# Cross-attention and FFN on one core: stacked 128-row score products, halves staged ahead, FFN by weight column groups

## The chip, the cores and the metric

One core of a Trainium2 chip runs the whole program. The metric is the device time of one launch in microseconds, and less is better. TensorE (PE) does matrix products into PSUM, VectorE (DVE), ScalarE (ACT) and GpSimd (POOL) do elementwise work, and SyncE (SP) issues nearly all transfers (DMA). Each engine takes its instructions in order and waits on semaphores.

## The reference

```
x = x + xattn(layernorm(x), ctx, mask, mask, Wq, bq, Wk, bk, Wv, bv)     # x: (16, 256, 512)
x = x + ffn(layernorm(x), lut, gate_idx, up_idx, down_idx)

xattn: 16 heads of 16 rows; q = Wq t + bq, k = Wk s + bk, v = Wv s + bv, each (16, 256, 512)
       dot = q.T k / 4 per head (512 x 512);  m = mask_t * mask_s
       amap = softmax(m * dot - (1 - m) * 1e6) * m;  out = amap v
ffn:   w = lut[idx] for gate, up (1376 x 512) and down (512 x 1376), lut of 16 entries
       out = (silu(x gate.T) * (x up.T)) down.T
```
All arrays are float32. The layer norm runs over the 512 columns. Rows of the FFN are the 16 x 256 rows of x.

## The kernel before

**Units and steps.** A group k (0 to 31) is half the heads of one batch: 8 heads of 16 rows. It has two units u = 2k + e, each with 4 heads (even or odd ones). A unit has 4 column chunks c of 128; a step is one chunk and two heads, so a unit is 8 steps and there are 512. At step s, `quad(a, p)` (L403 to L436) makes two score blocks of 128 x 1024: pa for a unit 12 steps ahead (AHEAD = 12), of which DVE takes the row maximum (L434), and pb, the transposed block of the unit at hand, of which ACT takes the exponential (L436). The three buffers of `ps_sc` are shared by pa and pb.

**A score block is three products.** TensorE's fast float32r form keeps fewer bits than float32, so q and k are cut into halves (high bits, rest). Each head has 32 rows: `qs`, `ks` hold (high, rest), `qx`, `kx` the swapped order. A block adds ks x qs, kx x qs and a product of mask rows (`ka`, `qa`), and for pb the rows `qm` with the maximum. Each product is 32 rows tall; two heads of pa and two of pb sit in four different row groups, and the order written out is n (product), jj (head), pa then pb.

**Staging.** `project` (L332 to L356) makes q or k of a group in float32, POOL multiplies the mask, `halve` (L250) cuts, and three transfers (L355) write the halves to a DRAM tile of 8 heads x 48 rows. `spread` (L358 to L370) reads them back: per unit four copies of 256 KB into 128 rows (L363, L364) and two of mask rows (L368). `turn_max` (L438 to L449) turns the maxima on TensorE and sends them to `qm` in four transfers (L448). `apply_v` (L452) multiplies by v in float32, 4 heads in 4 column groups, once every second step; of the 32 columns of a head 16 are ones and give the softmax sums.

**Rows.** `take_sums` (L478), `merge` (L484), `invert` (L488), `send_sums` (L493), `spread_sums` (L498, L504) and `finish_rows` (L510 to L512) bring the sums of a group together, divide, add x and write x2 to DRAM. All of these transfers, the staging, the loads of the next batch (`load_b`), of rows for the statistics of layer norm (`load_xs`, L233) and of the index tables (L559) are issued on SP's one queue, in the order of the step table (`after`, `lumps`, from L515).

**Order.** `manual_schedule` keeps the order as written. The table fixes at which step each piece stands; `fill_step` gives DVE a credit of 0.39 us of table look-ups per step, which turn the indices into the gate and up weights (`wg`, `wu`, kept in SBUF).

**FFN.** 8 blocks of 512 rows. `gate_up(n)` runs over 11 column groups o of the weights, 8 products of 128 x 128 x 512 in float32 each (two matmul records per product), Silu on ACT, a product on DVE; `down(n)` runs 4 x 11 products and adds x2. The rows of block n + 1 are normed and turned inside `gate_up(n)`. The down weights are looked up during the first two blocks. Block 0 starts beside the last attention steps.

Of the kernel before, what the change touches and what calls it, by code (L numbers as in the profile page):

```python
# [9 lines left out]
F32 = mybir.dt.float32  # L10
I32 = mybir.dt.int32
F32R = mybir.dt.float32r
HALF = -4096
# [8 lines left out]
def kernel(  # L22
# [17 lines left out]

# [15 lines left out]
    AHEAD = 12  # L70
    NSTEP = 8 * NU
    PIECE = INTER // 4
# [4 lines left out]
    wpool = ctx.enter_context(tc.tile_pool(name="ffnw", bufs=1))  # L77
    rpool = ctx.enter_context(tc.tile_pool(name="res", bufs=2))
    xpool = ctx.enter_context(tc.tile_pool(name="xT", bufs=1))
    dpool = ctx.enter_context(tc.tile_pool(name="dram", bufs=1, space=DRAM))  # L80
    ps_m = ctx.enter_context(tc.tile_pool(name="ps_m", bufs=1, space=PSUM))
# [3 lines left out]
    eps = cpool.tile([P, 1], F32, tag="eps", name="eps")  # L85
    nc.vector.memset(eps, EPS)
    lut_b = cpool.tile([P, LUT], F32, tag="lut", name="lut_b")
    lut_x = cpool.tile([P, LUT // 2], I32, tag="lutx", name="lut_x")
    wg = wpool.tile([P, NH, INTER], F32, tag="wg", name="wg")
    wu = wpool.tile([P, NH, INTER], F32, tag="wu", name="wu")  # L90
    x2_d = [dpool.tile([P, T], F32, tag=f"x2_{k}", name=f"x2_{k}") for k in range(NK)]

# [5 lines left out]
    def row_rstd(mv, rstd, nmr):  # L98

        nc.scalar.activation(rstd, mv[:, :, 1], AF.Sqrt, bias=eps)  # L100
        nc.vector.reciprocal(rstd, rstd)
        nc.vector.scalar_tensor_tensor(nmr, mv[:, :, 0], -1.0, rstd, ALU.mult, ALU.mult)

    lut_i = lut_b.bitcast(I32)

    def look_up(pool, dst, it, name):

# [7 lines left out]
        m, ops = [], []  # L115

        def low():
            m.append(new("b0"))
            v.tensor_scalar(m[0], it, 31, 31, ALU.logical_shift_left, ALU.arith_shift_right)

        def bit(i):
            m.append(new(f"b{i}"))
            v.tensor_scalar(m[i], it, 1 << i, None, ALU.bitwise_and)

        ops.append(low)
        for i in range(1, 4):
            ops.append(lambda i=i: bit(i))
# [10 lines left out]

        ops.append(lambda: leaf(0, d))
# [12 lines left out]
        ops.append(lambda: join(2, 4, 6))  # L152
        ops.append(lambda: join(3, 0, 4))
        return ops

    xTs, odd = {}, []

    def load_x2(pool, n, t):
        xt = pool.tile([P, T], F32, tag="x2", name=f"x2_{n}_{t}", bufs=4)
        nc.sync.dma_start(xt, x2_d[4 * n + t])  # L160
        return xt

    def prep_stats(pool, n):

        mv = pool.tile([P, 4, 2], F32, tag="mv", name=f"mv_{n}")
        rstd = pool.tile([P, 4], F32, tag="rs", name=f"rs_{n}")
        nmr = pool.tile([P, 4], F32, tag="nr", name=f"nr_{n}")
        xts = [load_x2(pool, n, t) for t in range(4)]
        for t in range(4):
            row_stats(pool, mv[:, t, :], xts[t], f"f{n}_{t}")  # L170
        row_rstd(mv, rstd, nmr)
        xTs[n] = (odd[0] if n % 2 else xpool).tile([P, NH, 4 * P], F32, tag="xT", name=f"xT_{n}")
        xns = {}

        def norm(t):
            xns[t] = pool.tile([P, T], F32, tag="xn2", name=f"xn2_{n}_{t}", bufs=2)
            nc.vector.tensor_scalar(
                xns[t], xts[t], rstd[:, t : t + 1], nmr[:, t : t + 1], ALU.mult, ALU.add
            )

        def turn(t):
            pt = ps_m.tile([P, 512], F32, tag="m", name=f"pt_{n}_{t}")
            xn = xns.pop(t)
            for h in range(NH):
                nc.tensor.transpose(
                    pt[:, h * P : (h + 1) * P], xn[:, h * P : (h + 1) * P], ident
                )
            nc.scalar.copy(
                xTs[n][:, :, t * P : (t + 1) * P], pt.rearrange("p (h r) -> p h r", r=P)
            )  # L190

        return norm, turn


    with ExitStack() as att:
        ac = att.enter_context(tc.tile_pool(name="att_const", bufs=1))
        p1 = att.enter_context(tc.tile_pool(name="att1", bufs=1))
        p2 = att.enter_context(tc.tile_pool(name="att2", bufs=2))
        pp = att.enter_context(tc.tile_pool(name="att_p", bufs=2))
        lp = att.enter_context(tc.tile_pool(name="lookup", bufs=1))  # L200
        ps_sc = att.enter_context(tc.tile_pool(name="ps_sc", bufs=3, space=PSUM))
        ps_pv = att.enter_context(tc.tile_pool(name="ps_pv", bufs=1, space=PSUM))

# [8 lines left out]
        m_d = dpool.tile([B, 4, T], F32, tag="m_d", name="m_d")  # L212
        mcomp = ac.tile([P, B, 32], F32, tag="mcomp", name="mcomp")
        mv1 = ac.tile([P, NK, 2], F32, tag="mv1", name="mv1")
        rstd1 = ac.tile([P, NK], F32, tag="rstd1", name="rstd1")
        nmr1 = ac.tile([P, NK], F32, tag="nmr1", name="nmr1")
        qss, qxs, kss, kxs = [
            [ac.tile([P, T], F32R, tag=f"{w}{i}", name=f"{w}{i}") for i in range(3)]
            for w in ("qs", "qx", "ks", "kx")
        ]  # L220
        qms = [ac.tile([P, T], F32R, tag=f"qm{i}", name=f"qm{i}") for i in range(3)]
        qas = [ac.tile([P, T], F32R, tag=f"qa{i}", name=f"qa{i}") for i in range(2)]
        kas = [ac.tile([P, T], F32R, tag=f"ka{i}", name=f"ka{i}") for i in range(2)]
        vas = [ac.tile([P, NCH, HEADS, 32], F32, tag=f"va{i}", name=f"va{i}") for i in range(2)]

        def x_of(b):
            return x[b].rearrange("(o p) t -> p o t", p=P)

        def load_xs(b):
            xs = []  # L230
            for o in range(NCC):
                t = p2.tile([P, T], F32, tag="xs", name=f"xs_{b}_{o}", bufs=1)
                nc.sync.dma_start(t, x_of(b)[:, o, :])  # L233
                xs.append(t)
            return xs

        def words(t):
            return t.bitcast(F32)

        def spread_mask(b):  # L240

            ka, qa = words(kas[b % 2]), words(qas[b % 2])
            for n in range(2):
                nc.sync.dma_start(ka[1 + n : P : 16, :], m_d[b, n].partition_broadcast(8))
                for h in range(2):
                    nc.sync.dma_start(
                        qa[1 + n + 16 * h : P : 32, :], m_d[b, 2 + h].partition_broadcast(4)
                    )

        def halve(hi, lo, t, eng):  # L250
            nc.vector.tensor_scalar(
                hi.bitcast(I32), t.bitcast(I32), HALF, None, ALU.bitwise_and
            )
            eng.tensor_tensor(lo, t, hi, ALU.subtract)

        def stats1(b, xs):
            for o in range(NCC):
                row_stats(p2, mv1[:, b * NCC + o, :], xs[o], f"a{b}_{o}")

        def rstd1_of(lo, hi):  # L260
            at = slice(lo * NCC, hi * NCC)
            row_rstd(mv1[:, at, :], rstd1[:, at], nmr1[:, at])
# [3 lines left out]
        def load_b(b):  # L266
            cx = p2.tile([P, NCC, T], F32, tag="ctx", name=f"ctx_{b}")
            nc.sync.dma_start(cx, src[b].rearrange("(o p) t -> p o t", p=P))
            xn = p2.tile([P, NCC, T], F32, tag="xn", name=f"xn_{b}")
            nc.sync.dma_start(xn, x_of(b))  # L270
            mb = p2.tile([P, T], F32, tag="mb", name=f"mb_{b}")
            nc.sync.dma_start(mb, mask[b, 0].partition_broadcast(P))
            inp[b] = (cx, xn, mb)

        def norm1(b, eng):
            xn = inp[b][1]
            for o in range(NCC):
                i = b * NCC + o
                eng.tensor_scalar(
                    xn[:, o, :], xn[:, o, :], rstd1[:, i : i + 1], nmr1[:, i : i + 1],  # L280
# [8 lines left out]
        nc.scalar.dma_start(bkc, bk.rearrange("(o p) -> p o", p=P))  # L289
        nc.scalar.dma_start(mrow, mask.rearrange("b o (c p) -> (b o c) p", p=P))  # L290
# [7 lines left out]
        for t in qms + qas:  # L298
            nc.gpsimd.memset(t.bitcast(F32), 0.0)
        for t in kas:  # L300
            nc.vector.memset(t.bitcast(F32), 0.0)
        ones = wg[:8, 3, :T]
        nc.vector.memset(ones, 1.0)
        for t in kas:
            nc.sync.dma_start(words(t)[0:P:16, :], ones)
        for t in vas:
            nc.gpsimd.memset(t, 1.0)
        stats1(0, [inp[0][1][:, o, :] for o in range(NCC)])
        rstd1_of(0, 1)
        norm1(0, nc.vector)  # L310
        nc.vector.tensor_scalar(bqc, bqc, QK, None, ALU.mult)
        mm = wg[:B, 0, :T]
        nc.scalar.dma_start(mm, mask[:, 0, :])
        for n, (by, op) in enumerate(((-1.0, ALU.add), (NEG, ALU.mult))):
            m, hi = wg[:B, 1 + n, :T], wg[:B, 1 + n, T : 2 * T]
            nc.vector.tensor_scalar(m, mm, by, None, op)
            halve(hi, m, m, nc.vector)
            nc.sync.dma_start(m_d[:, 2 * n, :], hi)
            nc.sync.dma_start(m_d[:, 2 * n + 1, :], m)
        spread_mask(0)  # L320
# [9 lines left out]
        nat, mbank = {}, {}  # L330

        def project(k, which, o):  # L332
            b, oc = divmod(k, NCC)
            cx, xn, mb = inp[b]
            w, src_t = (wk, cx) if which == "k" else (wq, xn)
            if o == 0:
                mbank[0] = ps_m.tile([P, 512], F32, tag="m", name=f"p{which}_{k}")
            nc.tensor.matmul(
                mbank[0], w[:, o, oc * P : (oc + 1) * P], src_t[:, o, :],
# [437 lines left out]
```

## Time and profile before

| what | us |
|---|---|
| median of 2 runs (2801.1 to 2802.07) | 2801.59 |
| the profiled execution | 2809.51 |
| its span, first to last instruction | 2807.7 |
| PE busy | 2148.9 |
| DVE busy | 1195.1 |
| ACT busy | 740.4 |
| POOL busy | 414.1 |

A page of the profile has the busy time of each engine, the same in 40 slices of 70 us (digits are tenths; PEclk is the clock granted to TensorE, DMA the busy share of the 16 DMA engines), the chain of waits that ended last, the costliest groups of instructions by line (count, then busy us and mean ns of one, then idle time ahead of them and what ended it), and the transfers. Groups name tiles: `pa<-ks,qs` writes pa from ks and qs. Float32 products of 128 rows pass at 8 records in 3.43 us when TensorE is full. The reduce of L434 takes 1222 ns each (512 of them), the exponential of L436 1023 ns (512).

### The profile page before, as it was taken

To read this page: it belongs to the slowest core of one execution; us is meant where nothing else is said; L and a number is where in the kernel's file an instruction comes from. 1 tells how busy PE (TensorE), PEld (TensorE's weight loads), DVE (VectorE), ACT (ScalarE), POOL (GpSimd) and SP (SyncE) were. 2 spreads that over 40 slices of the span, in tenths; PEclk is the share of its full clock that TensorE was granted. 3 is DMA by queue.
4 is the path that set the end of the run, shared out by engine and by line. 5 is a ranking of instruction groups with operands and counts; after the bars stand their busy time and mean duration, and the time that the engine had idled before them with its cause. 6 is when DMAs were issued, how large, how long until landed. Compare 5 with 4: busy or idle time off the path is not lost.

```text
span 2807.7 us, 28960 instructions
## 1 busy us (share of the span) xinstructions
PE 2148.9 (77%) x11009; PEld 926.4 (33%) x11009; DVE 1195.1 (43%) x1903; ACT 740.4 (26%) x892; POOL 414.1 (15%) x435
## 2 busy tenths in 40 slices
PE   1666655577677676767767667679999999999999
PEld 0322222233232232223223223233444444444444
DVE  2545455455455555555555555548811111111100
ACT  0233333243343333333333333341101011010100
POOL 2221111122122222212212222100000000000000
PEclk6677777788787877878878878899999999999999
DMA  3232333333333333333333332311011101011000
GB/s 118 84 107 91 121 105 92 107 93 110 115 91 114 109 91 107 106 97 111 104 103 107 93 114 91 97 59 34 26 38 38 45 0 45 12 34 45 4 26 15
DMA packets 135162, 217.83 MB, mean 78 GB/s; under 512 B 26736, under 2 KB 33840, under 8 KB 135024
## 3 DMA queue, kind: packets, MB, share of 16 engines
q1 hardware_dynamic: 133008, 214.73, 23.8%
q8 instruction: 87, 1.43, 0.2%
q10 hardware_dynamic: 1760, 0.99, 0.2%
q14 instruction: 51, 0.42, 0.0%
q0 software_dynamic: 256, 0.26, 0.0%
HBM read 140.26 MB, written 67.76 MB: 74 GB/s over the span
## 4 chain that ended last, share of the span: by engine, by line
PE 52%; DMA 31%; SPq 7%; DVE 4%; ACT 2%; issue 2%; POOL 2%; ACTq 0%; POOLq 0%; DVEq 0%
DMA qs<-dq 15%; PE po L697 11%; PE pg L679 10%; PE pu L679 10%; DMA dq<-natq 8%; PE pa L429 8%; PE pv L460 5%; DMA qx<-dq 4%; PE pb L429 3%; SPq L448 2%; PE pv L380 2%; SPq L355 1%; DMA xs<-in_x_dram 1%; ACT pt L436 1%; DVE nm L434 1%
## 5 line engine op out<-in xcount | busy, mean ns | idle before, releaser
L434 DVE TENSOR_REDUCE nm<-pa 128x2 f32<-128x1024 f32 x512 | 625.5, 1222 | 682.1 <-PE pb L429 526.3
L436 ACT ACTIVATE pt<-pb 128x1024 f32<-128x1024 f32 x512 | 523.6, 1023 | 1030.7 <-PE pb L429 866.9
L429 PE MATMUL pa<-ks,qs 32*128 32x512 f32 x1024 | 376.3, 575 | 509.4 <-DMA qs<-dq 435.7
L429 PEld LDWEIGHTS pa<-ks,qs 32*128 32x128 f32 x1024 | 168.1, 212 | 848.0 <-issue 641.9
L460 PE MATMUL pv<-pt,va 128*32 128x512 f32 x2048 | 350.1, 763 | 3.8 <-ACT pt L436 3.8
L679 PE MATMUL pg<-xT,wg 128*128 128x512 f32 (+1 forms) x704 | 320.8, 599 | 0.0
L679 PE MATMUL pu<-xT,wu 128*128 128x512 f32 (+1 forms) x704 | 316.5, 592 | 0.0
L429 PE MATMUL pb<-qs,ks 32*128 32x512 f32 x1024 | 297.0, 575 | 25.2 <-ACT pt L436 15.8
L429 PE MATMUL pa<-kx,qs 32*128 32x512 f32 x1024 | 313.9, 468 | 0.0
L429 PE MATMUL pa<-ka,qa 32*128 32x512 f32 x1024 | 307.0, 456 | 0.0
L697 PE MATMUL po<-wd,ht 128*128 128x512 f32 (+1 forms) x704 | 303.4, 592 | 0.0
L429 PE MATMUL pb<-qm,ka 32*128 32x512 f32 x1024 | 237.9, 457 | 54.3 <-DMA qm<-mx 54.3
L686 DVE TENSOR_TENSOR ht<-sg,pu 128x512 f32<-128x512 f32 (+1 forms) x88 | 60.4, 686 | 413.4 <-PE pu L679 410.3
L429 PE MATMUL pb<-qx,ks 32*128 32x512 f32 x1024 | 234.8, 452 | 0.0
L684 ACT ACTIVATE sg<-pg 128x512 f32<-128x512 f32 (+1 forms) x88 | 52.3, 596 | 650.0 <-PE pg L679 649.9
L697 PEld LDWEIGHTS po<-wd,ht 128*128 128x128 f32 (+1 forms) x704 | 133.7, 190 | 168.8 <-issue 168.8
L679 PEld LDWEIGHTS pu<-xT,wu 128*128 128x128 f32 (+1 forms) x704 | 132.1, 188 | 170.1 <-issue 169.6
L679 PEld LDWEIGHTS pg<-xT,wg 128*128 128x128 f32 (+1 forms) x704 | 131.6, 190 | 159.4 <-issue 158.2
L429 PEld LDWEIGHTS pa<-ka,qa 32*128 32x128 f32 x1024 | 176.4, 225 | 11.8
L389 POOL TENSOR_TENSOR vt<-vt,bvb 128x256 f32<-128x256 f32 x64 | 45.8, 739 | 906.4 <-ACT vt L386 906.4
L429 PEld LDWEIGHTS pa<-kx,qs 32*128 32x128 f32 x1024 | 152.0, 225 | 0.0
L702 DVE TENSOR_TENSOR ob<-po,x 128x512 f32<-128x512 f32 x32 | 22.1, 691 | 279.7 <-PE po L697 279.7
(96 smaller groups left out, 1883.1 us busy)
## 6 DMA issues: line engine op xcount, KB each, us to landing
dk<-hik SPq DMA_DIRECT2D x64, 256.0 KB
dq<-hiq SPq DMA_DIRECT2D x64, 256.0 KB
ks<-dk SPq DMA_DIRECT2D x64, 256.0 KB
kx<-dk SPq DMA_DIRECT2D x64, 256.0 KB
qs<-dq SPq DMA_DIRECT2D x64, 256.0 KB
qx<-dq SPq DMA_DIRECT2D x64, 256.0 KB
x<-x SPq DMA_DIRECT2D x64, 256.0 KB
ctx<-in_ctx_dram SPq DMA_DIRECT2D x16, 512.0 KB
```

Source lines behind the costliest of these rows:

```text
L355: nc.sync.dma_start(d[:, r : r + 16, :], f)
L380: nc.tensor.matmul(ps[:, i * C : (i + 1) * C], cx[:, o, c * P : (c + 1) * P], wv[:, o, :], start=(o == 0), stop=(o == NCC - 1),)
L389: nc.gpsimd.tensor_tensor(vt[:, cc], vt[:, cc], bvb, ALU.add)
L429: nc.tensor.matmul(ps[:, jj, :], w[at, cc * P : (cc + 1) * P], m[at, :], start=(n == 0), stop=(n == 2),)
L434: nc.vector.tensor_reduce(nms[u][:, c, h : h + 2], pa, AX.X, ALU.max, negate=True)
L436: nc.scalar.activation(pts[u2, c2][:, h2 : h2 + 2, :], pb, AF.Exp)
L448: nc.sync.dma_start(words(qms[u % 3])[0:P:16, c * P : (c + 1) * P], mx[8 * c : 8 * c + 8, :])
L460: nc.tensor.matmul(accs[u][32 * j : 32 * j + 32, :], va[:, c, 8 * oc + 2 * j + e, :], pt[:, j, :], start=(c == 0), stop=(c == NCH - 1),)
L679: nc.tensor.matmul(ps[:rows], w[:, h, at], xT[:, h, :], start=(h == 0), stop=(h == NH - 1),)
L684: nc.scalar.activation(sg[:rows], pg[:rows], AF.Silu)
L686: nc.vector.tensor_tensor(ht[:rows], sg[:rows], pu[:rows], ALU.mult)
L697: nc.tensor.matmul(po, ht[:rows, t * P : (t + 1) * P], wd[:rows, o, :], start=(o == 0), stop=(o == NO - 1),)
```

## The change

**Scores.** A head's rows are stacked to 128: rows 0 to 31 and 32 to 63 hold the halves, 64 to 67 the mask rows, 126 and 127 the two halves of the maximum; the rest is zero in Q and one in K. A block is then one product per head of 126 (pa) or 128 (pb) rows, 4 matmuls a step where there were 12. Q and K are four tiles each, of 128 x 4 x 512. pa and pb no longer alternate: pa's two, then pb's two. AHEAD is 14. `apply_v` runs two chunks every fourth step, with three `pt` buffers.

**Staging.** The high half is made by an ACT copy to float32r, the rest on POOL. `stage` writes a half in two transfers per group and side; `fetch_unit` reads a unit 8 steps before its first pa. `turn_max` sends two transfers, `take_sums` one, `send_sums` two.

**Layer norm.** Its root is a power on POOL, not Sqrt on ACT; statistics are taken from `load_b`'s own tile. Each group's rows are normed and turned inside the attention loop (`stats2`, `norm2`, `turn_rows`) and written to DRAM as `xT_d`.

**FFN.** Looked-up gate and up weights go to DRAM (`w_d`), half of the columns during attention (0.26 us of credit a step), the rest and the down weights during gate/up (3.8 us of credit per group and block). Gate/up runs over column groups o outside and row blocks n inside, with all 8 xT blocks in SBUF; each h piece is written to DRAM (`h_d`). All of the down products follow, with h loaded back two blocks ahead.

The core of the diff (new line numbers differ from those of the profile):

```diff
-    AHEAD = 12
+    AHEAD = 14
-        qss, qxs, kss, kxs = [
-            [ac.tile([P, T], F32R, tag=f"{w}{i}", name=f"{w}{i}") for i in range(3)]
...
+        Qs = [ac.tile([P, 4, T], F32R, tag=f"Q{i}", name=f"Q{i}") for i in range(4)]
+        Ks = [ac.tile([P, 4, T], F32R, tag=f"K{i}", name=f"K{i}") for i in range(4)]
...
-                for r, f in ((0, hi), (32, hi), (16, t)):
-                    nc.sync.dma_start(d[:, r : r + 16, :], f)
+        def stage(k, which):
+            d = dpool.tile([2, 2, D, 4, T], F32, tag=f"d{which}{k % 2}", name=f"d{which}_{k}")
+            hl = words(nat[which, k])
+            for a in range(2):
+                nc.sync.dma_start(d[a].rearrange("e p j t -> j (e p) t"), hl[:, a, :])
...
-                d = nat[which, k].rearrange("(j e) r t -> e j r t", e=2)[e]
-                nc.sync.dma_start(words(ss[u % 3]), d[:, 0:32])
-                nc.sync.dma_start(words(xs[u % 3]), d[:, 16:48])
+            dk = nat["k", k][:, e].rearrange("a p j t -> a p (j t)")
+            dq = nat["q", k][:, e].rearrange("a p j t -> a p (j t)")
+            for r in range(2):
+                nc.sync.dma_start(kt[32 * r : 32 * r + 32], dk)
+            for a in range(2):
+                nc.sync.dma_start(q[32 * a : 32 * a + 32], dq[a].partition_broadcast(2))
+            for t, r in ((q, 0), (kt, 4)):
+                nc.sync.dma_start(
+                    t[64:68],
+                    m_d[b, r : r + 4].rearrange("m (o t) -> m o t", o=1).to_broadcast([4, 4, T]),
+                )
...
+                for jj in range(2):
+                    j = h + jj
+                    nc.tensor.matmul(
+                        pa[:, jj, :], q[0:126, j, c * P : (c + 1) * P], kt[0:126, j, :],
+                        start=True, stop=True,
+                    )
...
+            at(t - 38, project, k, "k")
+            at(t - 34, project, k, "q")
+            at(t - 36, halve, k, "k")
+            at(t - 32, halve, k, "q")
+            at(t - 32, stage, k, "k")
+            at(t - 28, stage, k, "q")
+            at(t - 30, project_v, k)
+            at(t - 5, turn_max, 2 * k)
+            at(t + 3, turn_max, 2 * k + 1)
+            at(t - 22, fetch_unit, 2 * k)
+            at(t - 14, fetch_unit, 2 * k + 1)
+            at(t + 10, take_sums, k, 0)
+            at(t + 18, take_sums, k, 1)
+            at(t + 18, merge, k)
+            at(t + 20, invert, k)
+            at(t + 21, send_sums, k)
+            at(t + 23, spread_sums, k)
+            at(t + 26, finish_rows, k)
+            at(t + 28, stats2, k)
+            at(t + 30, norm2, k)
+            at(t + 38, turn_rows, k)
...
+        for o in range(NO):
+            for n in range(NB):
+                gate_up(o, n)
+                looked.fill(3.8)
+                if n == 3 and o + 1 < NO:
+                    load_w(o + 1)
+        looked.rest()
+        load_h(0)
+        load_h(1)
```
In the table t = 16 k is the first pb step of group k.

## The prediction

> **What bounds the kernel now.** I read the page first, then busy time by stage, then the chain of waits in order of time, then the SP queue's timeline inside a stall, and last the DMA share in stretches that hold one kind of transfer.
>
> ```profile
> PE   1666655577677676767767667679999999999999
> ...
> DMA  3232333333333333333333332311011101011000
> ...
> PE 52%; DMA 31%; SPq 7%; DVE 4%; ACT 2%; issue 2%; POOL 2%; ACTq 0%; POOLq 0%; DVEq 0%
> ```
> The left 26 slices are attention, with PE only 60 to 70% busy; the right ones are the FFN, with PE full. The chain is a third transfers.
>
> ```profile
> core 0: us, PE busy (x) PEld busy (x) DVE busy (x) ACT busy (x) POOL busy (x), PEclk, DMA share, GB/s
> 0.00:72.50 72.50, 9.86 (x17) 4.58 (x18) 17.59 (x39) 3.93 (x7) 19.97 (x31) 0.68 0.39 117
> 72.50:1861.70 1789.20, 1214.24 (x8769) 511.33 (x8769) 947.33 (x1435) 645.84 (x746) 391.62 (x402) 0.79 0.32 101
> 1861.70:2807.70 946.00, 924.81 (x2224) 410.52 (x2224) 230.22 (x429) 90.58 (x139) 2.53 (x2) 0.99 0.09 30
> ```
> Attention takes 1789 us for 32 groups of heads k, 56 each; no engine is full there. The FFN is 946 us with PE at 925: only less matmul would shorten it.
>
> ```profile
> 1241.62 1.27 SPq L355 DMA_DIRECT2D dq<-hiq  x2
> ...
> 1243.12 0.57 SPq L355 DMA_DIRECT2D dq<-natq  x1
> ...
> 1249.44 0.51 SPq L363 DMA_DIRECT2D qs<-dq  x1
> ...
> 1257.48 0.76 PE L429 MATMUL pa<-ks,qs 32*128 32x512 f32 x1 [10.93 <-DMA qs<-dq]
> ```
> ```profile
> PE pa L429 <- DMA qs<-dq: 435.7, 55, 23.8
> ```
> ```profile
> SPq L484 <- DMA qx<-dq: 64.5, 30, 2.3
> ```
> First the timeline (start, length): the halves go to DRAM at 1243, the copies back are issued at 1249 once they landed, and PE starts at 1257; it had stood 10.9 us. Then the waits (total us, times, longest): 436 us of that kind in all. The last line, of SP's own waits, is a queue limit: L484 (merge) uses nothing of qx. In the built program every SP transfer waits for the one eight places before it.
>
> ```profile
> 541.80:543.80 2.00, 2.00 (x16) 1.10 (x13) 1.64 (x3) 1.12 (x2) 0.00 (x0) 0.50 1.05 407
> 58.00:62.00 4.00, 0.00 (x0) 0.00 (x0) 0.00 (x0) 0.00 (x0) 0.00 (x0) 0.50 0.53 204
> 553.00:557.00 4.00, 0.00 (x0) 0.00 (x0) 0.00 (x0) 0.00 (x0) 0.00 (x0) 0.50 0.29 105
> 1250.80:1256.00 5.20, 0.00 (x0) 0.00 (x0) 0.00 (x0) 0.00 (x0) 0.00 (x0) 0.50 0.28 106
> ```
> This decides the forecast. The last two columns are the share of 16 DMA engines and GB/s. In the first stretch ctx and xn load, 128 rows on both sides: all engines, 407. In the second the dq writes run, DRAM side 8 groups of 16 rows: half, 204. In the last two qs and qx load, DRAM side 4 groups of 32 rows: about a quarter, 105, though qs and qx are both queued. So a transfer gets as many engines as its outermost dimension has entries, queued ones share the same engines, and each engine moves 407/16 = 25.4 GB/s.
>
> **The change, part by part.** *Fetch.* Per unit (8 steps) four copies of 256 KB stay, but their DRAM sides are now 2 groups of 16 rows of 8 KB (K: the two halves; Q: one half read twice). No row has two groups; by 8 and 4 I take two engines, 51 GB/s. Ends: 16 engines (0.65 us a copy) and two (5.15). I take two, since 8 to 4 already halved the rate. Four copies: 4 x 5.15 = 20.6; two mask copies of 32 KB over 4 engines 0.65; together 21.3, where qs, qx, ks and kx over 4 engines needed 10.3.
>
> The Trainium skill, "DMA: Bandwidth & Descriptors", section "Why a DMA increments its semaphore by 16 and not by 1", says that a copy uses the largest number of engines up to 16 that divides the slowest dimension of both sides. By it these copies get 2, and the sum stands. Its section "Bandwidth" gives 6.15 us for 1 MB to 128 partitions; with that for a fetch the sum would be, as an estimate, near 2320. No row here has two groups.
>
> *Stage.* hl goes out in four 256 KB copies per k (six before), DRAM side 4 groups: 2.6 us each on engines 0 to 3, 10.4 per k. *Small ones:* two sums transfers replace eight, mx goes in 4 transfers instead of 8; they also use engines 0 and 1 and so land behind a fetch. rb 1.3, xr, x2 and the new xT write 0.65 each, load_b 1.3 MB over 16 engines 3.2 every second k. On engines 0 and 1 a k comes to 2 x 21.3 + 10.4 + 1.3 + 1.9 + 1.6 + about 2 for small ones = 60: more than the whole 56 of before.
>
> *The period of one k*, from the SP order. Fixed cost of a transfer: xs issued at 20.79, used at 23.60, 256 KB at 407 GB/s being 0.65, so 2.2; I split it 1.3 ahead, 0.9 behind. Let the odd unit's fetch issue at 0.
> - Fetch to 22.6, stage q behind it to 27.8; send_sums 1.6 more with landing (dd at 1867.47, rb at 1869.00): 29.5. spread_sums is queued behind send_sums and waits for that landing.
> - rb: issue to POOL 3.8 (1869.00 to 1872.84), two POOL products 2.6, issue of x2 and sums 1.2: 37.1. Only then is the even unit's fetch issued; it stands behind finish_rows in SP's order.
> - That fetch 1.3 + 21.3, load_b 1.6 on average, landing 0.9: 62.2. The maxima mx are queued behind it, and pb of the even unit waits for them.
> - pb 1.1, two apply_v at the half clock after a stall 3.7 (a row of 1.94 each), us copy 0.6, sums 0.6, four merges 2.5 (x4 in 2.48), slack 0.1: 70.8. Then the next odd fetch.
>
> PE's new wait on mx holds all that stands behind it: pa and apply_v on PE, so reduce on DVE, exp on ACT, then the us copy, the merges on SP and the next fetch; that is why the last line above is paid in full. The fetch stands 8 steps ahead of its use, and its slot is free in time (pb of four units before ended some 20 us earlier), but it can't pass the SP transfers ahead of it. If mx did not queue behind the fetch, pb would start some 20 us earlier, but the same fetch would still be waited for by pa two steps later.
>
> PE needs 16 steps x 2.0 = 32 in a period and is hidden. The 2.0 lies between 1.25 (reduce of 1.22 alone) and 2.15 (exp at 1242.33, 1244.50, 1246.62). Of it: 12 matmuls of 32 rows in three sets 0.23 apart become 4 full ones, 0.92 at full clock if the 0.18 weight loads hide, 1.64 if not. DVE has 1.22 plus 0.45 of lookups and small work, ACT 1.02 plus 0.35, POOL 15 us per k. Eleven Sqrt table loads (14.1 us of ACT) go; all that is hidden by the fetches, and costs what rival 1 says if they are not there.
>
> *Start.* The statistics loads of three batches go (ACT stood 30.3 us for them). hl of k=0 is ready near 27 us (DVE memsets 7.8, POOL memsets to 17, norm 2.75, projection 2, POOL and ACT passes 3.9). Then engines 0 and 1 carry 10.4 + 21.3 + 3.2 + 5.2 + 21.3 + 5.2 + 21.3, 88, and 4 of fixed cost: first exp at 119, against 97.8.
>
> *Attention.* First odd fetch at 122, 30 periods of 70.8 = 2124, 10 for the lookup transfers: last odd fetch at 2256, landed at 2279. 24.5 steps x 2.0: 2328.
>
> *Tail.* The first FFN load now stands on SP behind the last xT write: last products and copy 3.8; copy to second POOL product 13.1 (1862.36 to 1875.44); statistics 2.0 (the two small POOL ops between 0.1 and 0.8 each); norm 0.8, turn and copy 1.8, write 2.8, then 1.5 MB at 407 GB/s 6.1: 30.4, at 2359. Before, gate_up(0) covered this.
>
> *FFN.* 88 gate/up groups of 16 records x 0.4293 = 6.87: 604.6 and 2 for a cold clock; per group DVE has 3.8 of lookups and 0.69, hidden under 6.87. h transfers move 256 KB per 6.87 us, hidden. The moving xT is read in four runs of 128: at the turn's rate (x4 in 0.44) a record takes 0.44, 15 us more in all; I take 0.4293, since those records also pay a weight load each. The turns and the stalls of before go (946 to 921). Handover: load_h stands behind the last h write: Silu 0.6, product 0.69 and their waits 1.5, issue 0.6, 2.6 MB at 407 GB/s 6.5, fixed 2.2, the last 96 rows and a cold clock 1.2: 12. Down 8 x 37.78 = 302.2; end 3.6.
>
> Sum: 2359 + 606.6 + 12 + 302.2 + 3.6 = 3284 span, against 2807.7. The profiled execution took 2809.5, 1.8 over its span and 7.9 over the median 2801.6: 3284 + 1.8 - 7.9 = **3278**.
>
> **Rivals.** *1, width is not set by the groups, all 16 engines:* a fetch is 2.6 + 2.2, nothing waits; exp at 69, 512 x 1.9 = 973, then 30.4 + 925: 1997. For it: 8 KB rows are longer than any seen. Against: three widths follow the groups. This is the one that ends faster; it decides once a fetch is below 12.7 us (a period of 54.9 gives 2802), so at more than three engines.
> *2, four engines is the floor:* fetch 11, period 50.1: 2620. Only two widths below 16 are seen, so it can't be excluded.
> *3, no handover costs:* engines 0 and 1 are never idle, period 60: 2950. Against: rb waits on the same queue that must issue the next fetch.
> *4, handovers cost more:* merges at 1.1 each (x4 in 4.43 when the queue is loaded) and 2 more per landing: period 79, 3525.
>
> **How the numbers follow.** Forecast (period 65 to 75) 58%, rival 3 15%, rival 4 12%, rival 1 9%, rival 2 4%, near no change 2%. Range 2930 to 3530, from rival 3 to rival 4; rivals 1 and 2 are left out. About 2% is what a measurement here can tell from no change. Faster 0.13, same 0.03, slower 0.84.
>
> **What would show it.** DMA share near 0.13 at 51 GB/s in a stretch with only K and Q copies; PE waiting on Q<-mx and K<-dk or Q<-dq; exps in bursts of 8 with 71 us per 16 steps; PE idle some 12 us between gate/up and down. Wrong if the share in such a stretch is 0.28 or more, or if steps run evenly at 2 us.

## The result, and the profile after

The changed kernel takes 3296.61 us (median of 2 runs, 3293.69 to 3299.52) against 2801.59: ratio 1.177, 95% interval 1.172 to 1.182. The prediction said 3278, a ratio of 1.170 where 1.177 was measured. The profiled execution took 3293.69 us, its span is 3291.9.

First the page of the changed kernel: TensorE and the DMA engines in 40 slices, then the chain by engine and by line.

```profile
PE   3544645554454555445455544554699999998999
...
DMA  3212121222212222221212222111422211114332
...
PE 43%; DMA 38%; DVE 6%; SPq 3%; issue 2%; POOL 2%; ACT 1%; POOLq 0%; DVEq 0%; ACTq 0%
DMA Q<-mx 26%; PE po L674 9%; PE pg L632 9%; PE pu L632 9%; DMA Q<-dq 8%; PE pv L438 6%; DVE nm L400 4%; PE pb L410 4%; PE pa L396 2%; PE pv L363 1%; PE pk L311 1%; SPq L344 1%; DVE hl L421 1%; POOL va L378 1%; SPq L346 1%
```
Attention fills 28 slices instead of 26, and they are longer (82.3 us instead of 70.2); PE is busy 40 to 60% in them, before 60 to 70%. Transfers hold 38% of the chain, before 31%, and two names carry it: the maxima (Q<-mx) and the Q copies.

By stage, the last columns being the granted clock, the share of the 16 DMA engines and GB/s. The first line is the kernel before, from its first pb product to its FFN; the others are the changed kernel (attention from its first pb, gate/up, down):

```profile
97.85:1861.70 1763.85, 1192.85 (x8681) 501.38 (x8680) 928.08 (x1408) 644.31 (x743) 383.02 (x392) 0.79 0.32 101
```
```profile
118.70:2336.00 2217.30, 1154.66 (x4705) 555.52 (x4705) 839.96 (x992) 673.82 (x813) 426.46 (x505) 0.77 0.21 73
...
2380.00:2984.00 604.00, 592.72 (x1382) 258.62 (x1380) 275.51 (x448) 51.31 (x86) 0.00 (x0) 0.99 0.20 68
2984.00:3292.00 308.00, 304.11 (x704) 134.15 (x704) 22.12 (x32) 0.00 (x0) 0.00 (x0) 0.99 0.31 117
```
From the first pb on, attention went from 1764 to 2217 us although PE's busy time in it fell from 1193 to 1155, with little more than half the matmul records. Up to the first pb it takes 118.7 us (before 97.9), the FFN with its lead-in 956 (946). Of the 484 us that the span grew, 453 lie in attention, 21 in the start and 10 in the FFN; PE's idle time in attention grew by 492. (The prediction's row of 1789 us begins at 72.5, with the first pa, not with the first pb.)

The stretch that decides, with K and Q copies alone on the queue, the waits of pb, and the SP queue over one period (start, length):

```profile
1205.00:1211.00 6.00, 0.09 (x1) 0.00 (x0) 1.35 (x3) 1.02 (x1) 5.61 (x10) 0.84 0.14 52
```
```profile
PE pb L410 <- DMA Q<-mx: 806.8, 62, 21.2
```
```profile
1203.63 1.36 SPq L344 DMA_DIRECT2D K<-dk  x2
...
1212.51 1.20 SPq L428 DMA_DIRECT2D Q<-mx  x2
...
1232.51 0.66 SPq L478 DMA_DIRECT2D rb<-dd  x1
...
1239.07 0.33 SPq L492 DMA_DIRECT2D x<-us  x1
...
1240.16 1.34 SPq L344 DMA_DIRECT2D K<-dk  x2
...
1243.73 1.22 SPq L428 DMA_DIRECT2D Q<-mx  x2
...
1270.37 2.48 SPq L460 DMA_DIRECT2D us<-us  x4
1272.95 1.36 SPq L344 DMA_DIRECT2D K<-dk  x2
```
Two engines of 16 work, at 52 GB/s. mx (two transfers of 8 KB) is issued at 1243.73, 3.6 us behind its fetch, and pb starts only at 1264.29: it waited 13.8 us for it there, 807 us in all. From one odd fetch to the next this period takes 69.3 us, on average 72.1 over the last 30 (71.2 between the merges that the table below counts).

### The profile page after: what moved, and what is told of

It is laid out like the page before. It is cut to its first block, busy times and chain, and to the rows that moved or that the text cites. A ratio compares the mean times of both kernels' runs of the same rounds, so it can differ in the third digit from the quotient of the medians.

```text
span 3291.9 us, 20238 instructions
## 1 busy us (share of the span) xinstructions
PE 2107.6 (64%) x6913; PEld 975.2 (30%) x6913; DVE 1178.4 (36%) x1528; ACT 741.4 (23%) x923; POOL 473.0 (14%) x562
## 4 chain that ended last, share of the span: by engine, by line
PE 43%; DMA 38%; DVE 6%; SPq 3%; issue 2%; POOL 2%; ACT 1%; POOLq 0%; DVEq 0%; ACTq 0%
DMA Q<-mx 26%; PE po L674 9%; PE pg L632 9%; PE pu L632 9%; DMA Q<-dq 8%; PE pv L438 6%; DVE nm L400 4%; PE pb L410 4%; PE pa L396 2%; PE pv L363 1%; PE pk L311 1%; SPq L344 1%; DVE hl L421 1%; POOL va L378 1%; SPq L346 1%
## 5 line engine op out<-in xcount | busy, mean ns | idle before, releaser
L410 PE MATMUL pb<-Q,K 128*128 128x512 f32 x1024 | 382.8, 460 | 883.6 <-DMA Q<-mx 806.8
L410 PEld LDWEIGHTS pb<-Q,K 128*128 128x128 f32 x1024 | 199.0, 213 | 1003.6 <-issue 834.6
L396 PE MATMUL pa<-K,Q 126*128 126x512 f32 x1024 | 401.1, 476 | 47.3 <-DMA K<-m_d 41.6
L674 PE MATMUL po<-wd,hs 128*128 128x512 f32 (+1 forms) x704 | 304.1, 595 | 11.4 <-DMA hs<-h 11.4
L396 PEld LDWEIGHTS pa<-K,Q 126*128 126x128 f32 x1024 | 188.2, 205 | 255.6 <-issue 198.2
L674 PEld LDWEIGHTS po<-wd,hs 128*128 128x128 f32 (+1 forms) x704 | 134.2, 191 | 181.4 <-issue 181.4
L490 POOL TENSOR_TENSOR us<-us,rb 128x512 f32<-128x512 f32 x32 | 41.1, 1284 | 867.3 <-issue 400.2
L327 POOL TENSOR_TENSOR hlq<-natq,hlq 128x512 fp32r<-128x512 f32 x32 | 40.8, 1276 | 636.9 <-ACT hlq L326 636.9
L438 PEld LDWEIGHTS pv<-pt,va 128*32 128x32 f32 x2048 | 68.5, 141 | 206.7 <-issue 203.4
L378 POOL TENSOR_SCALAR va<-vt,mcol 128x128 f32<-128x128 f32 x128 | 76.9, 618 | 0.0
```

The costliest lines, as they stand in the source:

```text
L327: nc.gpsimd.tensor_tensor(hl[:, 1, :], t, words(hl[:, 0, :]), ALU.subtract)
L378: nc.gpsimd.tensor_scalar(a4[:, e, :, 16 * e : 16 * e + 16], v4[:, e], m, None, ALU.mult)
L396: nc.tensor.matmul(pa[:, jj, :], q[0:126, j, c * P : (c + 1) * P], kt[0:126, j, :], start=True, stop=True,)
L410: nc.tensor.matmul(pb[:, jj, :], kt[:, j, c * P : (c + 1) * P], q[:, j, :], start=True, stop=True,)
L438: nc.tensor.matmul(accs[u][32 * j : 32 * j + 32, :], va[:, c, 8 * oc + 2 * j + e, :], pt[:, j, :], start=(c == 0), stop=(c == NCH - 1),)
L490: nc.gpsimd.tensor_tensor(u, u, rb, ALU.mult)
```

## The experiments

All are edits of the changed kernel. "Period" is from the merges of one group to those of the next, mean over groups 1 to 30. The kernel before took 2802 to 2807 us beside them. In some edited kernels the same statement stands a few lines further down.

| run | us | ratio to before, 95% | period, us |
|---|---|---|---|
| the changed kernel | 3296.6 | 1.177 [1.172, 1.182] | 71.2 |
| q_wide | 2935.6 | 1.047 [1.044, 1.050] | 60.3 |
| all_wide | 2427.9 | 0.866 [0.864, 0.867] | 44.6 |
| no_copies | 2395.9 | 0.855 [0.853, 0.857] | 41.6 |
| two_queues | 3150.6 | 1.125 [1.122, 1.127] | 66.4 |
| sums_late | 3245.2 | 1.157 [1.155, 1.160] | 69.6 |
| mx_own_queue | 3114.7 | 1.111 [1.108, 1.113] | 65.6 |
| wide_mx | 2518.1 | 0.898 [0.896, 0.900] | 47.2 |
| wide_mx_late | 2447.5 | 0.873 [0.872, 0.875] | 44.7 |
| wide_late | 2391.8 | 0.853 [0.851, 0.855] | 43.0 |
| wide_mx_pool | 2343.4 | 0.835 [0.833, 0.837] | 41.3 |
| best | 2381.1 | 0.848 [0.847, 0.850] | 43.2 |
| all_three | 2301.0 | 0.820 [0.819, 0.821] | 40.5 |

My theory going in: the width of the copies (two engines), times SyncE's order, makes the loss. The rivals: the bytes or the queue are slow whatever the width, or the handovers alone make the loss.

### Is it the number of outermost groups? q_wide and all_wide

The same bytes, transfers, queue and steps; only the order of Q's and K's 64 stacked rows differs, so that a copy's DRAM side has 16 groups of 2 rows instead of 2 of 16. all_wide:

```diff
-            dk = nat["k", k][:, e].rearrange("a p j t -> a p (j t)")
-            dq = nat["q", k][:, e].rearrange("a p j t -> a p (j t)")
+            dk = nat["k", k][:, e].rearrange("a p j t -> p a (j t)")
+            dq = nat["q", k][:, e].rearrange("a p (o j) t -> a p o (j t)", o=1)
...
-                nc.sync.dma_start(q[32 * a : 32 * a + 32], dq[a].partition_broadcast(2))
+                nc.sync.dma_start(
+                    q[32 * a : 32 * a + 32], dq[a].to_broadcast([D, 2, 4 * T])
+                )
```
q_wide widens Q alone; K goes to every second row, in 2 groups:

```diff
+            dq = nat["q", k][:, e].rearrange("a p j t -> p a (j t)")
...
+                nc.sync.dma_start(kt[r:64:2], dk)
...
+                nc.sync.dma_start(q[32 * a : 32 * a + 32], dq)
```


> The rows of Q and K are put in another order (the same in both, so the products are the same sums), so that the DRAM side of the two Q copies of a fetch has 16 groups of 2 rows outermost, and that of the two K copies still 2 groups of 16 rows. Bytes, transfers, queue and steps stay as in the changed kernel. My theory (a copy gets as many DMA engines as its DRAM side has outermost entries): the Q copies take 262144 bytes at the 407 GB/s of 128 rows, 0.64 us each, the K copies stay at 5.15, so a fetch takes 2 x 5.15 + 2 x 0.64 + 0.65 = 12.2 us instead of 21.3, about the break-even fetch of 12.7; the period of 16 steps falls by 1.85 x 9.1 = 17 us, and 30 periods by about 500: 2790 us, between 2740 and 2850, so the time of the kernel before within 2%. Rival (the bytes, the four-place queue or the shared rows are slow, not the outermost count): 3250 to 3300. Rival (the handovers grow with what the fetch gives back): above 2900.

> As q_wide, but all four copies of a fetch have 16 groups of 2 rows outermost on the DRAM side; nothing else differs from the changed kernel. My theory: a fetch takes 4 x 0.64 + 0.65 = 3.2 us instead of 21.3; by the same slope the period falls by 1.85 x 18.1 = 33 us to 38 and the kernel to 3297 - 30 x 33 = about 2290 us; if the other handovers of SyncE are then hidden too, TensorE's own step of 1.45 to 1.65 us (as measured after the last fetch) gives a period of 26 and 1920 us. Range 1900 to 2350, well below both kernels. Rival (bytes or queue, not the outermost count): 3250 to 3300. Rival (another bound right behind, for instance the stages with their 4 groups): 2500 or more.

Measured: 2935.6 and 2427.9. The rival "bytes or queue" is out: by row order alone 869 us went, and the kernel became 13% faster than the one before. A stretch of a fetch in all_wide (its SP queue issues K at 1279.64 and Q at 1280.93), and one of q_wide when only the K copies are left:

```profile
1281.00:1283.00 2.00, 1.18 (x6) 0.60 (x4) 1.66 (x2) 1.02 (x1) 1.86 (x3) 1.00 1.01 250
```
```profile
1268.00:1270.00 2.00, 0.00 (x0) 0.00 (x0) 1.92 (x4) 0.00 (x0) 1.71 (x2) 0.50 0.12 49
```
All engines work in the first, two in the second; so two groups again gave two engines, 16 gave 16. The first moved 250 GB/s, though, and not the 407 that my sums take for a wide copy: a fetch of 3.2 or 12.2 us was nowhere measured. The wait of pb for mx, with its fetch:

```profile
PE pb L410 <- DMA Q<-mx: 486.1, 54, 14.9
```
```profile
PE pb L412 <- DMA Q<-mx: 69.1, 16, 6.1
```
From 807 us to 486 (q_wide) and 69 (all_wide). But q_wide missed its range (2740 to 2850) by 86 us, and came out where its second rival stood (above 2900, the handovers grow with what the fetch gives back); all_wide missed its own range (to 2350) by 78, short of its rival's 2500. The period gives back less per us of fetch than I had summed. Where it goes is the next question.

### What do the steps take by themselves? no_copies

This kernel leaves out the K and Q copies of all units after the fourth:

```diff
+            if u < 4:
...
-            for r in range(2):
-                nc.sync.dma_start(kt[32 * r : 32 * r + 32], dk)
+                for r in range(2):
+                    nc.sync.dma_start(kt[32 * r : 32 * r + 32], dk)
```
(the Q copies likewise)

> The changed kernel without the four K and Q copies of every fetch after the fourth; the tiles keep the rows of the first four units, so the scores of later units are of the wrong heads, and everything else (masks, maxima, stages, sums, all steps) stays. It shows what the steps take when no fetch is in their way. Periods measured so far are 72.1 us with 21.3 us a fetch, 60.8 with about 12, 45.1 with about 3, so the time given back per us of copying is about 0.8 and not the 0.93 behind my break-even (1.85 a period of two fetches). My theory now: the steps themselves take about 40 to 44 us a period, not the 32 that I had counted as hidden, so nearly all of what all_wide still takes is steps: 2428 - 30 x 3 = 2340 us, between 2260 and 2420. Rival (the steps take 32 and the rest of all_wide's period is transfers): 2428 - 30 x 13 = 2040 us, below 2150.

Measured 2395.9, period 41.6: my theory then; the rival, 2040, is out. A stretch of its attention (200 to 1350 us), and the chain from 500 to 1300:

```profile
200.00:1350.00 1150.00, 898.60 (x4081) 456.09 (x4079) 741.83 (x881) 583.48 (x706) 391.19 (x461) 0.93 0.25 77
```
```profile
by line: DVE nm L401 20.5%; PE pv L439 16.4%; PE pb L411 11.7%; PE pa L397 10.8%; PE pv L364 4.1%; PE pq L311 4.0%; PE pk L311 3.4%; issue 3.2%; POOL va L379 2.9%; DMA dd<-den 2.7%; DVE hl L421 2.0%; DVE hl L422 1.8%; POOL vt L372 1.8%; DVE
```
PE is busy 0.78 of the time, 32.5 us of 41.6: that is my 16 x 2.0. But a step takes 2.6 us, not 2.0, with no fetch in its way. The chain says where: it goes from PE to the reduce on DVE (nm, its largest line) and back. That this handover is the whole difference was read from the chain; no run takes the reduce away. all_wide is 32 us above no_copies, 3 us a period. It is no floor for every order, since SyncE's other transfers stand where they stood: with all copies in place wide_mx_pool takes 41.3 a period and all_three 40.5 (both below).

### Two narrow copies on two queues: two_queues

```diff
-                nc.sync.dma_start(q[32 * a : 32 * a + 32], dq[a].partition_broadcast(2))
+                nc.scalar.dma_start(q[32 * a : 32 * a + 32], dq[a].partition_broadcast(2))
```


> The changed kernel with its narrow copies, but the two Q copies of a fetch go by ScalarE's queue, the two K copies by SyncE's as before. It tells whether two narrow transfers side by side on two queues use the same two engines or two each. Theory A (the n-th outermost entry goes to the n-th engine, whatever the queue, so all narrow copies share the same two engines): the fetch stays at 21 us, 3230 to 3310 us. Theory B (each queue deals its entries to engines of its own): a fetch takes 10.7 us, as in q_wide, 2850 to 3010 us. I hold A a little likelier, because the share of the engines was 0.14 (2.2 engines) with several copies of one queue outstanding.

Measured 3150.6, outside both ranges and between them, so the time alone decides nothing. In the trace Q's copies are issued by ScalarE at 1263.75 and K's by SyncE at 1264.32, and then:

```profile
1268.00:1274.00 6.00, 0.98 (x3) 0.86 (x4) 1.99 (x4) 0.26 (x1) 4.24 (x8) 0.53 0.12 52
```
Both queues have copies out (1 MB takes some 20 us at this rate), and the share is still two engines, 52 GB/s: theory A for the engines. The 146 us that it won anyway may come from the order on SyncE, where mx now stands behind two copies and not four (pb's wait for it is 664 us instead of 807); that part is only argued.

### Are the handovers a term of their own? sums_late

```diff
-            at(t + 23, spread_sums, k)
-            at(t + 26, finish_rows, k)
+            at(t + 28, spread_sums, k)
+            at(t + 31, finish_rows, k)
...
-            at(t + 28, stats2, k)
-            at(t + 30, norm2, k)
-            at(t + 38, turn_rows, k)
+            at(t + 33, stats2, k)
+            at(t + 35, norm2, k)
+            at(t + 41, turn_rows, k)
```


> The changed kernel with its narrow fetch, but the steps that hand the sums on come later (spread_sums by 5 steps, finish_rows, stats2 and norm2 by 5, turn_rows by 3), so that their transfers no longer stand ahead of a fetch while their own input is late. My theory: the 9.5 us a period that SyncE spends waiting there (29.5 to 37.1 of the period, and the issues) leave the path: 30 periods x 9 = 270 us less, 3030 us, between 2960 and 3100. Rival (the handovers lie beside the fetch and cost nothing): 3280 to 3310. Rival (the wait moves on to the next transfer of the queue): 3200 to 3300.

Measured 3245.2: 51 us, 1.6 a period, not 9. SyncE's waits, of this run:

```profile
SPq L492 <- POOL us L491: 268.8, 32, 10.0
SPq L518 <- ACT xt L517: 250.3, 31, 13.4
```
and of the changed kernel:

```profile
SPq L492 <- POOL us L491: 174.7, 32, 6.0
SPq L478 <- DMA dd<-den: 160.4, 31, 6.6
```
The wait for dd is gone (0.7 us); in its place SyncE waits longer for the rows (269 instead of 175 us) and 250 us for xt, where it had waited 5.9. The third line of the expectation hit: the wait moved to the next transfer that stood ahead of a fetch.

### Does mx stand behind the fetch? mx_own_queue, wide_mx, wide_mx_pool

```diff
-                nc.sync.dma_start(q[126 + h : 127 + h], mx[n * h : n * h + n, :])
+                nc.scalar.dma_start(q[126 + h : 127 + h], mx[n * h : n * h + n, :])
```


> The changed kernel with its narrow fetch, but the two transfers of the maxima (mx to Q's rows 126 and 127) go by ScalarE's queue and so no longer stand behind the fetch on SyncE's. My theory: pb starts while the fetch is still landing, so that the 8.6 us from the landing to the merges (pb, apply_v, the copy of us, the sums) go on beside it: period 62 to 63 instead of 71.9, 3297 - 30 x 9 = about 3030 us, between 2980 and 3120; the wait of pb for mx (807 us in 62 waits) nearly goes. Rival (the same fetch is waited for by pa two steps later and nothing is won): 3270 to 3310, with pa's wait larger by what pb's lost.

Measured 3114.7, on the upper edge: 182 us, 5.6 a period. pb's wait for mx fell from 807 us to 1.7, so mx did stand behind the fetch; part of it came back as pa's wait for the last copy of a fetch, its mask rows:

```profile
PE pa L396 <- DMA K<-m_d: 211.0, 30, 31.2
```
That line was 41.6 us in two waits in the changed kernel. pa's wait for the reduce also grew, from 5.5 to 214 us. Over the wide fetch:

> all_wide with the two transfers of the maxima on ScalarE's queue as in mx_own_queue. My theory: in all_wide the chain still holds about 3.6 us a period of mx landing behind a fetch, which goes: 2428 - 30 x 3.6 = about 2320 us, between 2280 and 2390. Rival (the steps are the bound, the wait was covered): 2400 to 2440.

Measured 2518.1: 90 us slower than all_wide. The wait that I meant to save did go (69 us, none left). On ScalarE, wide_mx:

```profile
1261.59 0.26 ACT L427 COPY mx<-pmx 32x128 f32<-32x128 f32 x1 [0.76 <-PE pmx L425]
1261.87 1.15 ACTq L430 DMA_DIRECT2D Q<-mx  x2
1263.07 1.02 ACT L416 ACTIVATE pt<-pb 128x1024 f32<-128x1024 f32 x1 [1.23 <-PE pb L412]
```
ScalarE issues for 1.15 us, and the exp stands behind it: its pb was done at 1262.48, and it starts at 1263.07, when the issuing ends. So the same edit with `nc.gpsimd`:

> wide_mx was 90 us slower than all_wide, against my expectation. My theory now: it is the issuing that costs; ScalarE, which the exps of every step wait for, issues four more transfers a period at 0.58 us each, 2.3 us x 32 = 74 us. Here they go by GpSimd's queue, which is busy a third of the time and off the path of the steps: 2330 to 2430 us. Rival (the maxima landing early changes the order of the steps for the worse, whichever engine issues): 2490 to 2540. Rival (GpSimd's own issuing is dear or its work is late by it): above 2540.

Measured 2343.4: 175 us less than by ScalarE, 85 less than all_wide. The two kernels differ in the issuing engine alone, so that decides, not that the maxima leave SyncE's queue. GpSimd issues hardly faster (1.03 to 1.11 us for the two, in five places of its trace). ScalarE's issuing time, 2.3 us a period, is less than half of the 6.0 between the two periods (47.2 and 41.3); the rest stays open.

### Putting together what won: wide_late, wide_mx_late, best, all_three

wide_late is all_wide with the edit of sums_late, wide_mx_late is wide_mx with it.

> wide_mx with the later steps of sums_late as well. My theory: with the fetch short, what waits behind a late handover is a larger part of the period than it was, and the chain of all_wide holds about 2.5 us a period of dd and rb: 30 x 2 = 60 us less than wide_mx, about 2260 us, between 2200 and 2340. Rival (as in sums_late the wait moves to the next transfer): within 25 us of wide_mx.

> all_wide (maxima on SyncE's queue) with the later steps of sums_late. With the narrow fetch those were worth 51 us, behind wide_mx 71. My theory: the same 60 to 70 us here, 2428 - 65 = about 2360 us, between 2330 and 2400; no_copies with 2396 is no floor for it, since that still has the early handovers. Rival (all_wide's period is steps alone and no handover is on the path): 2410 to 2440.

Measured 2447.5 (71 us off wide_mx; its rival is out, its range missed because wide_mx was dearer) and 2391.8 (36 us off all_wide, half of what I expected). So the later handovers are worth 51 us behind the narrow fetch, 36 and 71 behind wide ones: what they give doesn't follow the length of the fetch, and no run shows what it follows. best also loads h earlier:

```diff
+                if n == 3 and o + 1 == NO:
+                    load_h(0)
+                    load_h(1)
         looked.rest()
-        load_h(0)
-        load_h(1)
+        load_tail(0)
+        load_tail(1)
```
(`load_h` of blocks 0 and 1 loads ten column groups, `load_tail` the eleventh.)

> wide_late, and in the feed-forward part the loads of the first two h blocks' first ten column groups are issued inside the last column group instead of after it, and only the eleventh group's rows behind it. The handover between gate/up and down was 11.4 to 11.8 us in every run. My theory: it shrinks to 2 to 4 us: wide_late less 8 to 10 us. Rival (the large loads stand ahead of the last h stores on the queue and move the wait there): no change within 3 us, or slower.

Measured 2381.1, 10.7 us less than wide_late, and the line of po waiting for hs (11.4 us in the changed kernel) is no longer among the waits.

all_three is best with the maxima on GpSimd's queue.

> The three edits that each won something, together: the wide fetch, the maxima on GpSimd's queue, the later handovers, and the early loads of h. Alone, the later handovers took 36 us from all_wide, GpSimd's queue 84, the early loads 11 from wide_late. My theory: GpSimd's queue and the later handovers both take SyncE's waits off the same path, so of the 36 about half is left: 2343 - 18 - 11 = about 2315 us, between 2285 and 2335. Rival (they are worth their full sums): 2296 or less. Rival (the later steps of POOL now stand beside its issues and hold the maxima back): 2340 or more.

Measured 2301.0, 14 us below my number and near the full sums: 0.820 [0.819, 0.821] of the kernel before. Its chain:

```profile
PE 60%; DMA 17%; DVE 8%; POOL 7%; issue 4%; SPq 2%; ACT 2%; POOLq 0%; DVEq 0%; ACTq 0%
```

## Why the prediction was right, and where it was not

- **Two engines for a copy with two groups.** Right: 0.14 of the engines and 52 GB/s in the changed kernel (0.13 and 51 forecast), and by row order alone 1.01 of them in all_wide. This step carries the forecast. The Trainium skill's rule ("DMA: Bandwidth & Descriptors", section "Why a DMA increments its semaphore by 16 and not by 1"), that the slowest dimension of both sides sets the number of engines, agrees with these two numbers.
- **The period.** Right: 70.8 forecast, 72.1 between odd fetches. So rival 2 (four engines, 50.1) and rival 4 (dearer handovers, 79) are out. In the period shown above, from the odd fetch: rb at 28.9 (forecast 29.5), the even fetch at 36.5 (37.1), pb at 60.7 (62.2 and slack), the next odd fetch at 69.3 (70.8).
- **mx behind the fetch.** Right: 807 us of pb's wait, nearly all gone in mx_own_queue. "The same fetch would still be waited for by pa" was right in part: of 807 us 182 were won.
- **Start, tail, FFN.** First exp at 119.95 (119; the 97.8 set beside it is the first pb of before, whose first exp starts at 100.0); PE starts the FFN at 2366.8 (2359); gate/up to 2972.7, 605.9 (606.6); handover 11.4 (12); down 304.1 (302.2). In the tail, 1.5 MB at 407 GB/s are 3.9 us; the 6.1 comes out only with a fixed cost of 2.2, which isn't named there.
- **How near the total came.** The span is 8 us over the 3284, and part of that is luck: the first odd fetch came 9.4 us early (112.6 for 122), the 30 periods took 28 us more than forecast (2162.4 for 2134), and from the last odd fetch to the FFN it took 11 us less (91.8 for 103).
- **"PE needs 16 steps x 2.0 = 32 and is hidden."** PE's busy time was right (32.5 in no_copies), the conclusion for shorter fetches was not: the steps with their handovers take 41.6 in no_copies, so they come out from behind the fetch much earlier than I said. This is the term that was mis-sized. It did not touch the forecast, since the narrow fetch covers it.
- **Rival 1's time and the break-even.** Wrong, by the same term above all. All 16 engines give 2428 and not 1997; a fetch of about 12.2 gives 2936, where I had a break-even at 12.7. On a straight line between q_wide (12.2, by my sum) and all_wide (3.2) the break-even lies near 9.8 us, an estimate: 3.2 + 9.0 x (2802 - 2428) / (2936 - 2428). If the wide copies pass at the 250 GB/s of the stretch in all_wide, the two fetches take about 13.0 and 4.8 and the same line gives about 10.9.
- **The handover term, 29.5 to 37.1.** It is where I put it in the queue, but it isn't a price by itself: taken away it gave 1.6 of some 9 us a period. Rival 3 (no handover costs, 2950) was thus not tested cleanly by sums_late, since other waits took their place.

So the stacked product, the staging ahead and the new FFN order, taken together, do not make the kernel slower: with wide copies it takes 2428 us against 2802 to 2807. Its rows' order in the copies does: two groups outermost where there could be 16.

## What to carry to other kernels

Before a copy is made larger or fewer, read the outermost dimension of its DRAM side, and look in the trace at the DMA share while that copy is alone: here it told at once how many engines work (0.14 for two, 1.01 for all). In a queue that runs in order, a wait taken away may be worth only the distance to the next wait in it (51 us here where 270 were expected), so remove the long transfer first (869 us). And a sum that holds when one thing is slow says little of the time when that thing is fast; for the break-even, sum the path that comes out next with its handovers, not one engine's busy time.

## What the hardware showed that I had not expected

Copies on two queues had no more than two engines between them (0.12 of 16, 52 GB/s with both out). And it matters which engine issues: the same two 8 KB transfers a unit made the whole kernel 175 us slower by ScalarE's queue (2518.1) than by GpSimd's (2343.4), of which the issuing time would explain 74 (2.3 us x 32, an estimate). The granted clock over the span rose with the idle time's going: 0.828 in the changed kernel, 0.937 in all_wide, 0.960 in all_three.
